# A four-layer graph kernel on one core: the last row tile's products in row quarters of the array, and the degree products behind a conditional

## The chip, the cores and the metric

The kernel runs on one core of a Trainium2 chip. The metric is the device time of one execution in microseconds. The core's engines are named as the profile names them: PE is TensorE's matmul, PEld its weight load, DVE is VectorE, ACT is ScalarE, POOL is GpSimd, and SP is SyncE, which here issues most of the DMA loads. A q behind a name (PEq, SPq) means the engine's instruction sequencer.

## The reference, cut to what matters

The input is x (2708 rows of 256 numbers) and a square adjacency matrix of 2708 x 2708 numbers. Four layers follow, each made of a graph part and a feed-forward part, both added to x. The change touches the graph parts of layers 0, 1 and 2.

```python
# layer 0: a weight from every adjacency value
msg = layernorm(x) @ W + B
sens = exp(-(1/adj - 1)**2 / (2 * 0.5**2))
x = x + where(adj < 1, sens, 0) @ msg
# layer 1: an adjacency matrix that is scaled by the row sums on both sides
A = adj + eye
D = 1 / sqrt(sum(A, axis=1))
x = x + relu((A * D[:, None] * D[None, :]) @ (layernorm(x) @ W) + b)
# layer 2: attention over the neighbours
h = layernorm(x) @ W.T
s = where(scores > 0, scores, 0.2 * scores)   # scores = a_src[None, :] + a_dst[:, None]
e = exp(s) * (adj > 0)
x = x + elu((e / sum(e, axis=1)) @ h)
```

The feed-forward parts of layers 0 and 1 send rows to experts: two of eight in layer 0, one of eight in layer 1. Layer 3 has attention with four heads.

## The kernel before

**Tiles.** The 2708 rows are cut into 22 row tiles of 128; the last one, number FULL = 21, has only LAST = 20 rows. Q is 32, a quarter of the array. The adjacency matrix is read transposed (adjT), so that a block of 128 source rows and 128 target columns can stand as the stationary operand of a product.

**The graph parts.** In layers 0 and 1 the target tiles are taken in three groups (GROUPS of 9, 7 and 6 tiles, GROUPS1 of 8, 8 and 6; the last group's sixth is the target tile of 20 columns, which last_sums does for itself, in column quarters of the array). A group keeps its sums in PSUM, two target tiles to a bank (acc). A loop over the source row tiles j loads one stretch of adjT (adrow, five buffers in layer 0 and four in layer 1), makes weights of it, and multiplies each target tile's 128 columns with the 256 values of that row tile: msg in layer 0 (line 726), sup in layer 1 (line 942). In layer 0 the weights come from the helper weigh (line 699): three ScalarE activations and two VectorE instructions over the whole stretch. In layer 1 VectorE also writes the mask of nonzero entries (line 919) that layers 2 and 3 use. Layer 2 takes its target tiles in groups of 5, 5, 5, 4 and 2, one PSUM bank each; VectorE makes e from a row of factors, a column of factors G and the mask (line 1133), and TensorE multiplies it with hh, 257 columns wide (line 1136).

The row tile j = 21 goes through the same loop as the others, as its last step, with 20 rows in place of 128. After the loop the sums are read out of PSUM and added to x: line 748 in layer 0, grow (lines 907 to 913) in layer 1, result (line 1078) and a later grow in layer 2.

**The front of a layer.** In layer 0 front(t0) loads two row tiles of x and makes msg for them; it is called for every second j of the first group. In layer 1 norm_project goes through the row tiles in sets of 2, 4, 4, 4, 4 and 4 (FOURS): both loads the experts' outputs of layer 0 and adds them to x (line 846), stats and shift make mean and scale, ScalarE normalises, TensorE transposes and projects, and ScalarE scales the result by deg into sup (line 897). The tiles of both share their buffers with the adjacency rows of layer 1.

**The degrees.** While layer 0's experts run, VectorE adds up the adjacency rows into cs (line 784). Twenty-two products with a column of ones turn cs into deg (line 791), each followed by a VectorE copy (line 792). Before layer 1's front VectorE adds 1 and takes 1/sqrt by a shift and three Newton steps (rsqrt, line 147; called in line 851).

**The conditional.** The experts' rows are run in blocks. Fifteen of layer 0's later blocks always run; the rest stand in a conditional (run_rest, line 563), which in this data is not entered. Each engine takes its own branch there, and what follows the conditional and depends on work in it waits until the engine concerned has passed.

**The order of the work.** The framework traces the kernel and sets each engine's order of instructions by itself, by its own estimate of when each can start and by program order. Each engine then runs its own queue strictly in that order, SP's and POOL's too, so that a DMA that waits holds up those behind it. Where the author wants another order, a dependency without a semaphore is added by hand (tc.add_manual_dep with NoSync). A ScalarE activation through lnexp is tied in this way to the table of exp and log that pin loads.

The softmax here doesn't subtract the row's maximum and nothing guards it: scores larger than these inputs give would overflow.

## Time and profile before

| what | value |
|---|---|
| time of three runs, median (lowest to highest) | 2094.61 us (2092.79 to 2096.02) |
| the profiled execution: its own time | 2098.78 us |
| the profiled execution: span from first to last instruction | 2097.1 us |
| mean TensorE clock granted in it | 0.965 |
| products of the last row tile in layers 0, 1, 2 | 21 each |
| TensorE busy, its longest idle stretches | 1980.9 us; 13.3 us at 660, 10.7 us at 1210, 8.8 us at 2076, 8.7 us at 311, 7.9 us at 258 |
| DMA: bytes moved, mean rate | 226.64 MB, 108 GB/s |

The profile shows one execution on the chip. Its page gives each engine's busy time, the span in 40 slices, and groups of instructions by line, engine and operation, with the tiles they write and read. A float32 product appears as two records of PE and two of PEld. In a row of a group, the figures behind the count are the busy time in us and the mean duration of one record in ns, and behind the bar stands the engine's idle time before them with what ended it. In a row of waits the three figures are the total in us, the number and the longest. In a row of an engine's timeline the first figure is the start in us, the second the length.

### The profile page before, as it was taken

The numbers are of one execution on the slowest core, as the hardware profiler recorded it, in microseconds if no ns is written. First come the engines' busy times: TensorE is split into PE (matmuls) and PEld (weight loads), VectorE is DVE, ScalarE is ACT, GpSimd is POOL, SyncE is SP. The second block draws the span as 40 slices with busy tenths as digits, with TensorE's granted clock in tenths as the row PEclk, the third lists the DMA queues.
The fourth block names the chain that finished last, engine by engine and source line by source line (L and its number), as shares of the span: only waits on it lengthen the run. The fifth ranks groups of instructions, "written<-read, shape, count | busy, mean of one in ns | idle before, by whom it ended". The sixth has DMA issues, their size and how long they took to land.

```text
span 2097.1 us, 25890 instructions
## 1 busy us (share of the span) xinstructions
PE 1980.9 (94%) x9673; PEld 1424.7 (68%) x9673; DVE 1100.6 (52%) x2524; ACT 660.6 (31%) x1445; POOL 288.1 (14%) x315
## 2 busy tenths in 40 slices
PE   6999978999997999999899969999899999999997
PEld 5888767878885788878688848888566622232334
DVE  7677754544114323243331165455355488887876
ACT  7778732222222403022322351223243410120112
POOL 1004353333221000102142110000000000000000
PEclk9999989999997999999999989999899999999999
DMA  8435649987532442423265420000101000000000
GB/s 261 141 106 150 213 158 353 352 298 262 186 145 92 123 142 61 141 62 111 92 213 184 162 91 6 1 1 1 41 1 31 16 1 21 21 26 11 16 11 24
DMA packets 80611, 226.64 MB, mean 108 GB/s; under 512 B 15218, under 2 KB 38746, under 8 KB 71264
## 3 DMA queue, kind: packets, MB, share of 16 engines
q1 hardware_dynamic: 69056, 196.17, 28.4%
q0 software_dynamic: 11424, 28.74, 3.9%
q8 instruction: 80, 1.31, 0.3%
q14 instruction: 51, 0.42, 0.1%
HBM read 206.46 MB, written 20.65 MB: 108 GB/s over the span
## 4 chain that ended last, share of the span: by engine, by line
PE 57%; DMA 5%; issue 3%; DVE 2%; ACT 1%; POOL 1%; POOLq 0%; SPq 0%; DVEq 0%; ACTq 0%
PE num L1460 11%; PE ps_acc L1136 10%; PE acc L942 9%; PE ps_tmp L317 7%; PE den L1471 6%; DMA given<-ys,xs 4%; PE ps_acc L1312 3%; PE ps_tmp L238 3%; PE ps_acc L547 1%; PE ps_tmp L195 1%; PE ps_acc L238 1%; PE yacc L556 1%; PE ps_tmp L874 1%; DMA mine<-given 0%; POOL given L451 0%
## 5 line engine op out<-in xcount | busy, mean ns | idle before, releaser
L1455 DVE SCALAR_TENSOR_TENSOR e<-arena,G,mask 128x1024 f32<-128x1024 f32 (+2 forms) x264 | 294.1, 1149 | 44.0 <-PE den L1471 43.6
L556 PE MATMUL yacc<-wb,hTs 128*128 128x256 f32 x1152 | 267.5, 385 | 11.2 <-DVE ys L558 10.7
L556 PEld LDWEIGHTS yacc<-wb,hTs 128*128 128x128 f32 x1152 | 218.0, 193 | 44.0 <-DVE ys L558 14.6
L1460 PE MATMUL num<-e,wh 128*64 128x512 f32 (+4 forms) x1056 | 243.6, 558 | 0.0
L726 PE MATMUL acc<-msg,wt 128*128 128x256 f32 (+1 forms) x924 | 210.7, 386 | 7.9 <-DVE wt L704 7.9
L942 PE MATMUL acc<-sup,adrow 128*128 128x256 f32 (+1 forms) x924 | 214.4, 390 | 0.0
L1136 PE MATMUL ps_acc<-hh,e 128*128 128x257 f32 (+1 forms) x924 | 211.2, 386 | 0.0
L726 PEld LDWEIGHTS acc<-msg,wt 128*128 128x128 f32 (+1 forms) x924 | 175.7, 193 | 35.9 <-DVE wt L704 8.3
L942 PEld LDWEIGHTS acc<-sup,adrow 128*128 128x128 f32 (+1 forms) x924 | 176.6, 195 | 30.6 <-issue 5.5
L1136 PEld LDWEIGHTS ps_acc<-hh,e 128*128 128x128 f32 (+1 forms) x924 | 173.8, 193 | 29.6 <-issue 2.5
L547 PE MATMUL ps_acc<-xTs,wa 128*128 128x256 f32 x768 | 179.6, 385 | 8.7 <-DVE xTs L520 8.6
L1460 PEld LDWEIGHTS num<-e,wh 128*64 128x64 f32 (+1 forms) x1056 | 74.3, 138 | 155.2 <-issue 120.8
L549 ACT ACTIVATE hTs<-ps_acc,wa 128x256 f32<-128x256 f32 x192 | 89.9, 473 | 271.5 <-PE yacc L556 194.4
L547 PEld LDWEIGHTS ps_acc<-xTs,wa 128*128 128x128 f32 x768 | 142.1, 192 | 36.4 <-DVE xTs L520 11.4
L196 ACT COPY xT<-ps_tmp 128x256 f32<-128x256 f32 x126 | 43.0, 362 | 325.1 <-PE ps_tmp L195 324.0
L1471 PE MATMUL den<-e,wh 128*32 128x512 f32 (+4 forms) x1056 | 137.9, 551 | 0.0
L1133 DVE SCALAR_TENSOR_TENSOR e<-Rb,G,mask 128x640 f32<-128x640 f32 (+2 forms) x110 | 85.2, 775 | 97.1 <-PE ps_acc L1136 96.9
L451 POOL DMA_INDIRECT taken<-xr,r_ix x66 | 76.8, 1163 | 357.9 <-DVE b_vec L387 190.7
L451 POOL DMA_INDIRECT given<-ys,xs x72 | 81.8, 1136 | 229.9 <-DVE ys L559 166.0
L465 POOL DMA_INDIRECT xs<-taken,b_ix x72 | 87.2, 1212 | 189.0 <-DVE xTs L520 87.2
L919 DVE TENSOR_SCALAR mask<-adrow 128x1024 uint8<-128x1024 f32 (+1 forms) x66 | 41.6, 631 | 134.5 <-DMA adrow<-in_adjT 132.6
L558 DVE TENSOR_TENSOR ys<-yacc,wb 128x256 f32<-128x256 f32 x72 | 30.3, 421 | 155.2 <-PE yacc L556 155.0
(388 smaller groups left out, 2459.7 us busy)
## 6 DMA issues: line engine op xcount, KB each, us to landing
adhalf<-in_adjT SPq DMA_DIRECT2D x42, 677.0 KB
wb<-in_L_ffn_W2p SPq DMA_DIRECT2D x24, 1152.0 KB
wb<-in_L_ffn_Wdp SPq DMA_DIRECT2D x24, 1152.0 KB
wa<-in_L_ffn_W1b SPq DMA_DIRECT2D x24, 1028.0 KB
adrow<-in_adjT SPq DMA_DIRECT2D x42, 512.0 KB
adrow<-in_adjT SPq DMA_DIRECT2D x42, 320.0 KB
adrow<-in_adjT SPq DMA_DIRECT2D x21, 576.0 KB
adrow<-in_adjT SPq DMA_DIRECT2D x21, 448.0 KB
```

What stands on the lines that cost most here:

```text
L317: te.matmul(p[:, :w], lhsT=w1[:, c, f * P : (f + 1) * P], rhs=xnT[:, c, c0 : c0 + w], start=(c == 0), stop=(c == DC - 1))
L451: i = g.indirect_dma_start(out=dst, out_offset=bass.IndirectOffsetOnAxis(ap=ix, axis=0), in_=src, in_offset=None, bounds_check=bound, oob_ ...
L465: i = g.indirect_dma_start(out=dst, out_offset=None, in_=src, in_offset=bass.IndirectOffsetOnAxis(ap=ix, axis=0), bounds_check=bound, oob_ ...
L547: te.matmul(p[:, f % 2, :], lhsT=w1[:, c, f * P : (f + 1) * P], rhs=xT[:, c, :], start=(c == 0), stop=(c == DC - 1))
L549: s.activation(hT[:, f, :], p[:, f % 2, :], AF.Gelu, bias=bias[:, f : f + 1])
L556: te.matmul(q[:, k, :], lhsT=hT[:, f, k * P : (k + 1) * P], rhs=w2[k][:, f, :], start=(f == 0), stop=(f == HC - 1))
L726: te.matmul(p[:q, n - pair[0], :], lhsT=wt[:, k : k + q], rhs=msg[:r, j, :], start=(j == 0 and n == pair[0]), stop=(j == NT - 1 and n == p ...
L942: te.matmul(p[:q, n - pair[0], :], lhsT=ad[:, k : k + q], rhs=sup[:r, j, :], start=(j == 0 and n == pair[0]), stop=(j == NT - 1 and n == p ...
L1136: te.matmul(p[:q, : D + 1], lhsT=e[:r, k : k + q], rhs=hh[:r, j, :], start=(j == 0), stop=(j == NT - 1))
L1455: v.scalar_tensor_tensor(e[:r, :w], Rb[:r, k, :w], G[:r, j, 2 * pair + k, :], mask[:r, j, c0 : c0 + w], op0=ALU.max, op1=ALU.mult)
L1460: te.matmul(num[k * DK : (k + 1) * DK, hf, :q], lhsT=wh[:r, j, 2 * pair + k, :DK], rhs=e[:r, h0 - c0 : h0 - c0 + q], start=(j == 0), stop= ...
L1471: te.matmul(den[z : z + Q, :q], lhsT=wh[:ri, i, 2 * pair + k, DK : DK + 1].to_broadcast([ri, Q]), rhs=e[:ri, h0 - c0 : h0 - c0 + q], start ...
```

## The change

The last row tile is taken out of the common loop's shape. Its 20 rows are laid into the four row quarters of the array (rows 0, 32, 64 and 96), so that products of different target tiles, in different PSUM banks, stand in different quarters.

- spread_out copies the 20 rows of values to all four quarters, by four small products with the identity and one ScalarE copy. It is called for msg, for sup, and for hh and G.
- last_rows sets a tile to ones by a GpSimd memset and loads the 20 adjacency rows into quarters of it by DMAs on SP.
- last_product is one product in a row quarter; by_turns orders the target tiles so that neighbours lie in different banks.
- In layer 0 the last rows' weights and products stand in the middle of a group: ahead of row tile 19 in the first group, and of row tile 12 in the other two. The weights are taken over 384 or 256 columns of 128 partitions in place of 1152, 896 or 640 columns of 20. The front of the last two row tiles is called two steps earlier.
- In layers 1 and 2 they stay the last step of a group, with all rows of the mask filled.
- The degree products are ordered behind the conditional. They write one bank (a second one for the last tile), and ScalarE makes 1/sqrt(1 + d) as exp(-0.5 ln(1 + d)).
- In layer 1's front, the additions of a set's expert outputs are ordered behind the shift of the set before.

```diff
-        v.scalar_tensor_tensor(nb, st[0][:, :, 0], -1.0, st[1], op0=ALU.mult, op1=ALU.mult)
+        i = v.scalar_tensor_tensor(nb, st[0][:, :, 0], -1.0, st[1], op0=ALU.mult, op1=ALU.mult)
+        shifts.append(i.ins.name)
...
+    def spread_out(values):
+
+        n = values.shape[1]
+        p = ps_tmp()
+        for z in range(0, P, Q):
+            te.matmul(p[z : z + Q, :n], lhsT=ident[:LAST, :Q], rhs=values[:LAST, :], start=True,
+                      stop=True, tile_position=(0, z))
+        s.copy(values, p[:, :n])
+
+    def last_rows(dst, parts):
+
+        g.memset(dst, 1.0)
+        for q, k, c0, w in parts:
+            nc.sync.dma_start(dst[q * Q : q * Q + LAST, k : k + w],
+                              a["adjT"][FULL * P :, c0 : c0 + w])
+
+    def last_product(p, q, weights, k, values, stop=True):
+        te.matmul(p, lhsT=weights[q * Q : q * Q + LAST, k : k + P],
+                  rhs=values[q * Q : q * Q + LAST, : p.shape[1]], start=False, stop=stop,
+                  tile_position=(q * Q, 0))
+
+    def by_turns(own):
+
+        return [(n, t, k) for z in range(2) for n, (t, k, _) in enumerate(own) if n % 2 == z]
...
-            for j in range(NT):
+
+            places = {n: (n // 2 % 4, n // 8 * 2 + n % 2) for n in range(len(own))}
+            begin = tiles is GROUPS[0]
+            for j in range(FULL):
...
-                if tiles is GROUPS[0] and j % 2 == 0:
-                    front(j)
+                if begin and j % 2 == 0:
+                    for t0 in (j,) if j < FULL - 3 else (j, j + 2) if j == FULL - 3 else ():
+                        front(t0)
+                if begin and j == FULL - 2:
+                    spread_out(msg[:, FULL, :])
+                if j == (FULL - 2 if begin else 12):
+                    cols = [gp.tile([P, GMAX * P], F32, name=name, tag=name, bufs=bufs)[
+                        :, : (1 + max(k for _, k in places.values())) * P]
+                            for name, bufs in (("adrow", 5), ("y", 3), ("wt", 4))]
+                    last_rows(cols[0], [(places[n][0], places[n][1] * P, c0 + n * P,
+                                         min(2, len(own) - n) * P) for n in range(0, len(own), 2)])
+                    weigh(*cols, P)
+                    for n, t, _ in by_turns(own):
+                        last_product(acc[n // 2][:, n % 2, :], places[n][0], cols[2],
+                                     places[n][1] * P, msg[:, FULL, :], False)
...
-        for t in range(NT):
-            r = rows(t)
+
+        for q, t0, t1 in ((P, 0, FULL), (LAST, FULL, NT)):
             d = ps_tmp()
-            te.matmul(d[:r, :1], lhsT=cs[:, t * P : t * P + r], rhs=ones, start=True, stop=True)
-            v.tensor_copy(deg[:r, t : t + 1], d[:r, :1])
+            for t in range(t0, t1):
+                i = te.matmul(d[:q, t : t + 1], lhsT=cs[:, t * P : t * P + q], rhs=ones,
+                              start=(t == t0), stop=(t == t1 - 1))
+
+                tc.add_manual_dep(i.ins, scattered["given0"][-1].name, mybir.DependencyInfo(
+                    mybir.DependencyClass.NoSync, mybir.DependencyReason.DATA), reason="order")
+            lnexp(deg[:q, t0:t1], d[:q, t0:t1], AF.Ln, bias=ones[:q])
+        lnexp(deg, deg, AF.Exp, scale=-0.5)
...
-                        v.tensor_tensor(xs, xs, o[:r, some[0] - t0 : some[-1] + 1 - t0,
-                                                  k * D : (k + 1) * D], ALU.add)
-
-
-        v.tensor_scalar(deg, deg, 1.0, None, op0=ALU.add)
-        deg = rsqrt(tp, deg, NT)
+                        i = v.tensor_tensor(xs, xs, o[:r, some[0] - t0 : some[-1] + 1 - t0,
+                                                      k * D : (k + 1) * D], ALU.add)
+                        if shifts:
+
+                            tc.add_manual_dep(i.ins, shifts[-1], mybir.DependencyInfo(
+                                mybir.DependencyClass.NoSync, mybir.DependencyReason.DATA),
+                                reason="order")
...
+                if j == FULL:
+
+                    r = P
+                    if tiles is GROUPS1[0]:
+                        spread_out(sup[:, FULL, :])
                 ad = gp.tile([P, 8 * P], F32, name="adrow", tag="adrow", bufs=4)[:r, :w]
-                nc.sync.dma_start(ad, a["adjT"][j * P : j * P + r, c0 : c0 + w])
+                if j < FULL:
+                    nc.sync.dma_start(ad, a["adjT"][j * P : j * P + r, c0 : c0 + w])
+                else:
+                    last_rows(ad, [(q, 0, c0, w) for q in range(P // Q)])
...
+                if j == FULL:
+                    for n, t, k in by_turns(own):
+                        last_product(acc[n // 2][:, n % 2, :], n // 2, ad, k, sup[:, FULL, :],
+                                     n == pairs[n // 2][-1])
+                    continue
...
+            spread_out(hh[:, FULL, :])
+            spread_out(G[:, FULL, :])
...
-                    r = rows(j)
+                    r = P
...
-                    for (t, k, q), p in zip(own, acc):
-                        te.matmul(p[:q, : D + 1], lhsT=e[:r, k : k + q], rhs=hh[:r, j, :],
-                                  start=(j == 0), stop=(j == NT - 1))
+                    for n, ((t, k, q), p) in enumerate(zip(own, acc)):
+                        if j == FULL:
+                            last_product(p[:, : D + 1], n % 4, e, k, hh[:, FULL, :])
+                        else:
+                            te.matmul(p[:, : D + 1], lhsT=e[:, k : k + q], rhs=hh[:, j, :],
+                                      start=(j == 0), stop=False)
```

## The prediction, made before the result was known

> **What bounds the kernel now.** I began with the page's busy shares and its 40 slices.
>
> ```profile
> PE 1980.9 (94%) x9673; PEld 1424.7 (68%) x9673; DVE 1100.6 (52%) x2524; ACT 660.6 (31%) x1445; POOL 288.1 (14%) x315
> PE   6999978999997999999899969999899999999997
> PEclk9999989999997999999999989999899999999999
> ```
>
> TensorE is the bound nearly everywhere; its thin slices (6th, 13th, 24th, 29th, counted from 1) are the joints between stages. So I priced TensorE's time stage by stage, then asked at each joint what comes last. Next, the groups of instructions with shapes kept apart: the last row tile's products, and two of the products that already lie in column quarters.
>
> ```profile
> L726 PE MATMUL acc<-msg,wt 20*128 20x256 f32 x42 | 9.9, 383 | 0.0
> L942 PE MATMUL acc<-sup,adrow 20*128 20x256 f32 x42 | 10.9, 410 | 0.0
> L1136 PE MATMUL ps_acc<-hh,e 20*128 20x257 f32 x42 | 10.4, 387 | 0.0
> L256 PE MATMUL acc<-sup,adlast 128*32 128x256 f32 x42 | 2.8, 381 | 0.0
> L256 PE MATMUL ps_tmp<-hh,es 128*32 128x257 f32 x42 | 4.4, 529 | 0.0
> ```
>
> Two records are one product. 21 products on 20 rows take about 10 us, though they do a sixth of the work; 21 in column quarters take 2.8. The last row, the same work, takes 4.4. Fine windows (columns: stretch, its length, PE, PEld, DVE, ACT, POOL busy, clock, DMA) say why:
>
> ```profile
> 781.70:785.10 3.40, 3.40 (x16) 2.67 (x16) 2.55 (x4) 0.00 (x0) 0.00 (x0) 1.00 0.55 158
> 785.10:791.90 6.80, 6.80 (x17) 4.91 (x16) 6.80 (x16) 0.00 (x0) 0.00 (x0) 0.50 0.27 80
> 1358.60:1362.00 3.40, 3.40 (x16) 2.43 (x14) 2.09 (x10) 0.96 (x3) 0.00 (x0) 1.00 0.00 0
> 1362.00:1365.40 3.40, 3.40 (x8) 2.73 (x9) 3.16 (x12) 3.40 (x11) 0.00 (x0) 0.50 0.00 0
> ```
>
> The first and third stretch hold the last row tile's products at the end of a group. Right behind them the clock is 0.50, for 6.8 and 3.4 us, although TensorE was never idle. The same follows at 126.3, 904.6, 1307.4 (this slows the 4.4 us row) and 1413.2: 27.2 us at half clock, 13.6 us lost. Full rate is 3.40/16 = 0.2125 us per record, so 0.43 a product.
>
> Third, the joint of layers 0 and 1: SP's waits, the conditional's instructions, TensorE's timeline.
>
> ```profile
> SPq L56 <- DMA given<-ys,xs: 41.5, 1, 41.5
> SPq L56 <- PEq L565: 5.9, 1, 5.9
> ```
> ```profile
> L565 PEldq COMPARE_BRANCH  x2: 328/1992/3657, 660.2 to 1206.9; - x2
> L565 PEldq EVENT_SEMAPHORE  x2: 51/51/51, 664.0 to 1210.2; - x2
> ```
> ```profile
> 653.27 6.71 PE L791 MATMUL ps_tmp<-ones,cs 128*128 128x1 f32 x36 [0.24 <-DVE deg L792]
> 673.30 0.69 PE L195 MATMUL ps_tmp<-ident,xn 128*128 128x128 f32 x2 [13.32 <-ACT xn L207]
> ```
>
> TensorE does the degree products until 660.0, takes its branch at 660.2 (3.66 us), passes at 664.0, and only then SP loads the expert outputs; the scattered rows had landed 5.9 us before. TensorE then idles 13.32 us.
>
> **What the Trainium skill says.** "TensorE: Matmul & The Clock Gate", Part 3: K=32 products at different row positions run beside each other, four measured at 3.07 times one; a weight load overlaps a running product only if the row group differs. The trace has column quarters only: 21 products of 0.43 in 2.71 us, 3.3 times; it agrees for columns, and shows nothing for rows. "TensorEngine Tiling (Array Packing)", Key Properties: changing the mode drains TensorE; between the den and num products of layer 3 this costs 0.13 us (16 records, four steps of 0.43, took 1.85). The first page, Part 1, gives idleness as the cause of a half clock; the trace differs: a busy array with 20 rows in use gets it too. "Runtime: NRT & Kernel Launch", Instruction fetch mechanics: a taken branch outside the loaded window waits for a fetch; the 3.66 us agrees.
>
> **The change, part by part.**
>
> Products: per group the longest quarter holds 3, 2, 2 (layer 0, of 9, 7, 5), 2, 2, 2 (layer 1, of 8, 8, 5) and 2, 2, 2, 1, 1 (layer 2, of 5, 5, 5, 4, 2): 21 steps for 63 products, 42 x 0.43 = 18.1 us less. Bounds: from all four beside each other to none; I take all, as for columns. Each of 11 runs adds a mode change in and out, 0.26. Each spreading copy of 256 columns adds 0.43 + 0.26 = 0.7; its ScalarE copy (362 ns in L196's row) lies beside products. The quarters fill 80 rows for about 1 us, so I expect no half clock. Now by stage.
>
> Layer 0, group 1: 9 products 3.9 become 1.3 + 0.26, half a 3.5 us slow stretch returns 1.75, spreading takes 0.7: 3.4 less. Group 2: 3.0 becomes 1.1: 1.9 less. The narrower weights relieve ScalarE and VectorE, which have cover (75 and 72 us of 95). Group 3 ends on a DMA: its last rows come behind the expert weights in SP's queue, and ScalarE waits 9.73 us for them until 261.5; TensorE then does ten products in 6.4 us, at half clock. Behind the landing only five remain, 4.3 us, 2.1 less; the gathers for the experts come next, so I count 1.5. The weights' issue hangs on group 2's end and moves with it. Layer 0: 6.8.
>
> What moves: the last two tiles' front in group 1 goes from the last step but one to two steps sooner, with its two column loads (about 0.4 us each on SP; the rows of x were read long before, by 34 us) ahead of two adjacency loads, and some 2.2 us of VectorE work; with five row tiles buffered this costs nothing, and without that cover 1 to 2 us once. The last rows' own load and weights leave each group's end for its middle. In layers 1 and 2 VectorE now works on 128 instead of 20 rows, at the same price (L1133: 884 against 872 ns at 640 columns).
>
> The memsets: 204 ns for 128 columns, 314 for 260, so about 1.0 us for 1024; the four or five added loads, 0.35 us each on SP. Queued behind them on SP: the next rows' loads. Five buffers (four in layer 1) are some 10 us ahead, so I count nothing; without that cover each run costs 3 to 5 us.
>
> Degrees: TensorE ends the experts' outputs 0.5 earlier, at about 652.2, its branch runs meanwhile, and the last scatter, free of the degree copies, goes 0.6 earlier. SP then starts at 658.2 - 0.6 = 657.6 instead of 664.1: 6.4. The 22 products take 22 x 0.37 = 8.1 us (36 records in 6.71) in TensorE's idle time, and three ScalarE instructions about 0.8: done near 662, while the first sup comes near 669. Twenty-two copies and the VectorE root are off the path. Ordering: in the old order an addition that waits 0.95 for its load (0.69 itself) stands before the first group's last statistics; this returns 1.5. It gives back: additions now wait for the shift, a chain of about 6 us per four tiles against 5 or less, so the layer's first adjacency loads, in buffers shared with those tiles, come 2.8 earlier and not 7.9. In the 5.1 between, TensorE does 2.6 tiles of front (1.95 each) of 1.09 us work: 2.8. Joint: 5.6.
>
> Layer 1: in L910's records the four bank reads start at 783.2, 784.5, 786.3 and 788.1. Old boundary: 781.7 to 791.9 for the last products and the next row. New: all banks stop at 782.8, the fourth is read by 788.5, its products end 789.4: 2.5 less, twice. The end gives 0.3, spreading takes 0.7: 4.6.
>
> Layer 2: first boundary 1304.0 to 1311.2, 7.3, becomes 1.1 + 2.8: 3.4. Second and third: 6.2 each become 4.8, bound by the banks' reads: 2.8 together. Last two 0.4; two spreadings 1.1: 5.5.
>
> Sum: 6.8 + 5.6 + 4.6 + 5.5 = 22.5. The profiled execution took 2098.8 (span 2097.1): 2076.3. It lies 4.2 above the median of the runs, 2094.6; on that, 2072.
>
> **The rivals.**
>
> Half packing: the two passes of one product hold the next back, so two at a time. 63 x 0.215 = 13.5 instead of 9.0: 2076.5. For it: no row position is in the trace. Against: four column quarters start within 0.02 us.
>
> The clock stays: TensorE waits some 3 us at layer 1's boundaries and 1 in layer 2, enough for half clocks again. Four stretches of 3.4, half lost, 7 with layer 1's second window: 2079.
>
> No packing: products take their turns. What remains is the joint, 5.6, against 11 x 0.26 + 3.2 of spreading: 2094, no change.
>
> Slower: a memset stands on GpSimd behind indirect DMAs that wait for VectorE. GpSimd's timeline has such stretches in just these groups:
>
> ```profile
> 170.88 1.20 POOL L451 DMA_INDIRECT taken<-xr,r_ix  x1 [22.63 <-issue]
> 970.87 1.62 POOL L451 DMA_INDIRECT taken<-xr,r_ix  x1 [101.74 <-DVE b_nb L398]
> ```
>
> If layer 0's second memset, due near 150, goes behind the scatters that end at 199.8, SP's loads stop and TensorE runs dry from about 165: some 40 us, 2112. It decides once GpSimd delays a memset by more than the 10 us cover; at 23 us over the cover the gain is gone. Against: the memset's buffer is free 20 us before these scatters.
>
> **How the numbers follow.** Forecast 0.62 (own range 2062 to 2080: layer 0's end may give 2.4 more, the joint 2.3 more or 2 less, boundaries 3 either way); half packing 0.11, clock 0.13, no packing 0.06, slower 0.08. The range 2061 to 2086 leaves out the last two and the forecast's tails. A measurement of this kernel tells about 0.2%, 4 us, from no change: faster 0.86, same 0.06, slower 0.08.
>
> **What would show it.** Last-row groups with 21 products in some 3 us; clock 1.00 behind group ends; SP's first expert-output load at about 6 us behind the last scatter, no wait for PEq; VectorE's grow as the new wait at layer 1's boundaries. I am wrong if row quarters start one after another, if GpSimd's memsets end what SP waits for, or if the additions' new order holds the front.

## The result, and the profile after

The kernel after took 2085.78 us (median of four runs, 2082.76 to 2086.45) beside 2093.73 us for the kernel before: a ratio of 0.9958, with a 95% interval of 0.994 to 0.9975. That is 8 us less. The forecast was 22.5 us less. Measured again, with 22 executions beside 52, the same two kernels gave 0.998 (0.9967 to 0.9993), 4 us less. So the change is a small gain, a fifth to a third of the forecast.

The page of the kernel after, the first two of the rows shown before:

```profile
PE 1954.2 (94%) x9705; PEld 1403.3 (67%) x9705; DVE 1092.2 (52%) x2490; ACT 659.0 (32%) x1452; POOL 298.6 (14%) x321
PE   6999878999997999999899969999899999999997
```

TensorE is 27 us less busy, yet the spans of these two executions differ by 12.5 (2097.1 and 2084.6). So it waits more. The groups of instructions say that the products themselves did what was forecast (columns as before):

```profile
L286 PE MATMUL acc<-msg,wt 20*128 20x256 f32 x42 | 3.8, 409 | 0.5 <-ACT msg L276 0.5
L286 PE MATMUL acc<-sup,adrow 20*128 20x256 f32 x42 | 3.4, 401 | 0.6 <-issue 0.6
L286 PE MATMUL ps_acc<-hh,e 20*128 20x257 f32 x42 | 4.8, 420 | 0.0
L259 PE MATMUL ps_tmp<-hh,es 128*32 128x257 f32 x42 | 2.8, 382 | 0.0
```

The 63 last products take 12.0 us in place of 31.2. The mean of one record is as long as before (401 to 420 ns), and the sum of a group is a third to a half: the records lie over each other. These are the forecast's own sums: 7, 6 and 8 steps of 0.43 us, with 0.26 for each of 3, 3 and 5 runs, make 3.8, 3.4 and 4.7. The last row of the fence took 4.4 us before, because it fell into a half-clock stretch. The fine windows behind the first group's end of layer 1, and behind that of layer 2 (columns: stretch, its length, the busy time of PE, PEld, DVE, ACT and POOL, the clock, the DMA share, GB/s):

```profile
775.60:779.00 3.40, 3.02 (x7) 2.49 (x8) 3.40 (x7) 0.00 (x0) 0.00 (x0) 0.50 0.62 184
779.00:782.40 3.40, 3.40 (x17) 2.96 (x17) 3.40 (x6) 0.00 (x0) 0.00 (x0) 1.00 0.00 0
1299.80:1303.20 3.40, 3.40 (x49) 1.70 (x45) 3.09 (x15) 2.62 (x8) 0.00 (x0) 1.00 0.00 0
1303.20:1306.60 3.40, 2.73 (x11) 1.45 (x10) 3.40 (x15) 3.40 (x13) 0.00 (x0) 1.00 0.00 0
```

In layer 2 the clock stays at 1.00; in layer 1 one window of 3.4 us at half clock is left of two. The joint of layers 0 and 1, from the timeline:

```profile
646.39 6.58 PE L838 MATMUL ps_tmp<-ones,cs 128*128 128x1 f32 x44 [0.76 <-PEq L595]
651.46 21.44 SPq L56 DMA_DIRECT2D both<-given  x11
659.09 0.69 PE L198 MATMUL ps_tmp<-ident,xn 128*128 128x128 f32 x2 [6.12 <-ACT xn L210]
```

SP starts its loads 4.7 us behind the start of the last scatter (646.76), while TensorE is still at the degree products, and TensorE's idle stretch ahead of layer 1 is 6.12 us where it was 13.32. All this is as forecast. (The 6 us among the prediction's signs was a slip: its own sum, SP at 657.6 and the scatter at 653.2, gives 4.4.) Four waits were not forecast.

First, the end of layer 0, in the kernel after and then in the kernel before:

```profile
240.21 0.35 SPq L650 DMA_DIRECT2D wa<-in_L_ffn_W1b  x1
242.60 2.29 SPq L748 DMA_DIRECT2D adrow<-in_adjT  x2
259.43 0.83 ACT L141 ACTIVATE y<-adrow,tiny 128x640 f32<-128x640 f32 x1 [11.27 <-DMA adrow<-in_adjT]
264.18 5.97 PE L772 MATMUL acc<-msg,wt 128*128 128x256 f32 x20 [10.51 <-DVE wt L734]
```
```profile
266.25 6.46 PE L726 MATMUL acc<-msg,wt 128*128 128x256 f32 x20 [7.91 <-DVE wt L704]
```

Behind the experts' weights SP still issues two row tiles, now tiles 19 and 20 where it was 20 and 21. Ten products (20 records) still follow the landing, and in these two executions TensorE restarts 2.1 us earlier than before (266.25), not 6.8.

Second, the second group's end of layer 1. The lines are the last products, VectorE's first read of a bank (L964), its first xr (L182; xr is the tile of normalised rows for the feed-forward part), and TensorE's transposes of xr; first in the kernel after, then in the kernel before (there the first line is a row of a group):

```profile
890.75 1.15 PE L286 MATMUL acc<-sup,adrow 20*128 20x256 f32 x16
891.92 1.29 DVE L964 TENSOR_TENSOR o<-acc,deg 128x512 f32<-128x512 f32 x2 [1.16 <-PE acc L286]
905.62 2.67 DVE L182 TENSOR_SCALAR xr<-x,mv,rs_y 128x256 f32<-128x256 f32 x8 [0.24 <-DVE rs_y L158]
906.09 1.11 PE L198 MATMUL ps_tmp<-ident,xr 128*128 128x128 f32 x4 [3.19 <-DVE xr L182]
```
```profile
L942 PE MATMUL acc<-sup,adrow 20*128 20x256 f32 x16 | 4.2, 418 | 0.0
902.68 0.69 DVE L910 TENSOR_TENSOR o<-acc,rs_y 128x512 f32<-128x512 f32 x1 [1.16 <-PE acc L942]
916.58 2.68 DVE L182 TENSOR_SCALAR xr<-x,mv,rs_y 128x256 f32<-128x256 f32 x8 [0.31 <-DVE rs_y L158]
918.41 0.60 PE L195 MATMUL ps_tmp<-ident,xr 128*128 128x128 f32 x4
```

VectorE's chain from the first read to xr is 13.7 us after and 13.9 before: no shorter. Nor does it start sooner. Before, the last products start at 901.52 and run one after another; VectorE reads the first bank 1.16 us later, when that bank's two products are done and the others still run. After, all four banks are done at once, and the first read comes 1.17 us behind the start of the products. So the packing shortens TensorE's part by 3 us and leaves VectorE's where it was.

Before, TensorE was still at products when xr was ready (no wait at 918.41). After, it is through with them and waits 3.19 us, and the clock is half from 905.3 to 912.1. The half clock of the kernel before, from 904.6 on, had hidden a part of this wait: the kernel with layer 0's change alone (below), whose layer 1 is as before, met no half clock at this group's end and waited 1.79 us for xr already.

Third, the third group's end, after and then before:

```profile
989.19 0.66 PE L548 MATMUL turned<-ident,xs 128*128 128x128 f32 x4
989.29 1.29 DVE L964 TENSOR_TENSOR o<-acc,deg 128x512 f32<-128x512 f32 x2 [2.98 <-PE acc L286]
996.24 0.65 DVE L550 COPY xTs<-turned 128x512 f32<-128x512 f32 x1
996.94 4.79 PE L577 MATMUL ps_acc<-xTs,L_ffn_W 128*128 128x256 f32 x12 [7.10 <-DVE xTs L550]
```
```profile
998.58 0.69 DVE L910 TENSOR_TENSOR o<-acc,rs_y 128x512 f32<-128x512 f32 x1 [4.34 <-PE acc L942]
1005.63 0.65 DVE L520 COPY xTs<-turned 128x512 f32<-128x512 f32 x1
1006.33 3.78 PE L547 MATMUL ps_acc<-xTs,L_ffn_W 128*128 128x256 f32 x8 [5.78 <-DVE xTs L520]
```

The rows gathered for the experts are there in time; TensorE has turned them before 990. It waits for VectorE's copy of the turned rows, which stands in VectorE's queue behind this group's reads, growing and statistics: 6.95 us from the first read to the copy after, 7.05 before. It is the same pattern as at the second group's end. (An expectation below speaks of a wait for the gathered rows; the lines show otherwise.)

Fourth, layer 1's experts, after and then before:

```profile
1050.82 1.01 POOL L481 DMA_INDIRECT given<-ys,xs  x1 [0.30 <-issue]
1053.45 0.49 DVE L537 MEMSET xs<- 128x516 f32 x1 [7.40 <-DMA given<-ys,xs]
1054.45 0.68 DVE L550 COPY xTs<-turned 128x512 f32<-128x512 f32 x1
1055.18 1.79 PE L577 MATMUL ps_acc<-xTs,L_ffn_W 128*128 128x256 f32 x4 [3.17 <-DVE xTs L550]
```
```profile
1062.13 1.13 PE L547 MATMUL ps_acc<-xTs,L_ffn_W 128*128 128x256 f32 x4 [0.46 <-DVE xTs L520]
```

VectorE stands at a memset until a scatter of GpSimd has ended, with the copy that TensorE needs behind it. Before, that wait of TensorE was 0.46 us. (The scatter comes late because six other indirect DMAs stand ahead of it on GpSimd.)

One profiled execution has its own luck with the clock, so I set the stages beside each other over all profiled executions of this study whose code in that stage is that of the kernel before, or that of the kernel after (2 to 4 and 5 to 10 executions). "Half" is what the half clock costs (half of TensorE's busy time in such stretches), "work" is the rest of its busy time. Differences, after less before, in us:

| stage | length before -> after | difference | idle | half | work | forecast |
|---|---|---|---|---|---|---|
| start to the first expert product of layer 0 | 280.0 -> 276.9 | -3.1 | +6.8 | -4.9 | -4.9 | -6.8 |
| layer 0's experts | 374.7 -> 374.5 | -0.2 | +1.6 | -1.6 | -0.2 | 0 |
| to the first transposes of layer 1 | 19.9 -> 13.5 | -6.4 | -6.4 | +0.2 | -0.2 | with the next two |
| layer 1's graph part | 325.4 -> 328.0 | +2.6 | +6.4 | +0.5 | -4.4 | |
| layer 1's experts | 210.2 -> 216.1 | +5.9 | +4.0 | +2.1 | -0.2 | -10.2 for the three |
| to the first product of layer 2 | 46.6 -> 47.4 | +0.8 | +0.1 | +0.8 | 0 | with the next |
| layer 2's products | 215.6 -> 212.4 | -3.2 | +3.1 | -3.0 | -3.4 | -5.5 for the two |
| to layer 3's products | 199.5 -> 199.8 | +0.3 | +0.8 | -0.4 | -0.1 | 0 |
| layer 3's products (unchanged) | 397.9 -> 395.0 | -2.9 | 0 | -3.1 | +0.1 | 0 |
| to the end | 24.6 -> 25.2 | +0.6 | +0.4 | +0.2 | 0 | 0 |

The sum is -5.6 us, between the two measured differences. TensorE's work fell by 13.3 us; the forecast's own terms say 18.1 - 11 x 0.26 - 2.5 = 12.7. The clock returned 9.2. But TensorE's idle time grew by 23 us outside the joint. In the first row idle time took more than the saved work (6.8 for 4.9); what is left there is clock, and the three executions before stand anywhere between 276.1 and 283.6.

### The profile page after: what moved, and what is told of

Read it like the earlier page. It is cut to its first block, busy times and chain, and to the rows that moved or that the text cites. A ratio compares the mean times of both kernels' runs of the same rounds, so it can differ in the third digit from the quotient of the medians.

```text
span 2084.6 us, 25984 instructions
## 1 busy us (share of the span) xinstructions
PE 1954.2 (94%) x9705; PEld 1403.3 (67%) x9705; DVE 1092.2 (52%) x2490; ACT 659.0 (32%) x1452; POOL 298.6 (14%) x321
## 4 chain that ended last, share of the span: by engine, by line
PE 38%; DMA 5%; issue 3%; DVE 2%; ACT 1%; POOL 1%; POOLq 0%; DVEq 0%; SPq 0%; ACTq 0%
PE num L1532 11%; PE ps_acc L1208 9%; PE den L1543 6%; DMA given<-ys,xs 4%; PE ps_tmp L347 4%; PE ps_acc L1384 3%; PE ps_tmp L241 2%; PE ps_acc L241 1%; PE ps_tmp L198 1%; DMA mine<-given 0%; POOL given L481 0%; POOL xs L495 0%; DVE e L1202 0%; PE ps_tmp L1461 0%; DMA arena<-rows 0%
## 5 line engine op out<-in xcount | busy, mean ns | idle before, releaser
L586 PE MATMUL yacc<-wb,hTs 128*128 128x256 f32 x1152 | 266.8, 384 | 12.5 <-DVE ys L588 12.4
L586 PEld LDWEIGHTS yacc<-wb,hTs 128*128 128x128 f32 x1152 | 217.0, 192 | 45.4 <-DVE ys L588 17.1
L772 PE MATMUL acc<-msg,wt 128*128 128x256 f32 x882 | 199.5, 383 | 12.4 <-DVE wt L734 11.7
L1009 PE MATMUL acc<-sup,adrow 128*128 128x256 f32 x882 | 200.5, 385 | 1.5 <-DVE o L964 1.5
L1208 PE MATMUL ps_acc<-hh,e 128*128 128x257 f32 x882 | 199.2, 382 | 1.7 <-ACT o L1153 1.7
L772 PEld LDWEIGHTS acc<-msg,wt 128*128 128x128 f32 x882 | 165.8, 191 | 38.7 <-DVE wt L734 13.0
L1009 PEld LDWEIGHTS acc<-sup,adrow 128*128 128x128 f32 x882 | 166.5, 192 | 28.8 <-issue 4.5
L1208 PEld LDWEIGHTS ps_acc<-hh,e 128*128 128x128 f32 x882 | 163.7, 190 | 29.3 <-ACT o L1153 4.7
L481 POOL DMA_INDIRECT given<-ys,xs x72 | 87.7, 1218 | 229.1 <-DVE ys L589 163.0
```

Source lines behind the costliest of these rows:

```text
L481: i = g.indirect_dma_start(out=dst, out_offset=bass.IndirectOffsetOnAxis(ap=ix, axis=0), in_=src, in_offset=None, bounds_check=bound, oob_ ...
L586: te.matmul(q[:, k, :], lhsT=hT[:, f, k * P : (k + 1) * P], rhs=w2[k][:, f, :], start=(f == 0), stop=(f == HC - 1))
L772: te.matmul(p[:q, n - pair[0], :], lhsT=wt[:, k : k + q], rhs=msg[:r, j, :], start=(j == 0 and n == pair[0]), stop=(j == FULL - 1 and n == ...
L1009: te.matmul(p[:q, n - pair[0], :], lhsT=ad[:, k : k + q], rhs=sup[:r, j, :], start=(j == 0 and n == pair[0]), stop=False)
L1208: te.matmul(p[:, : D + 1], lhsT=e[:, k : k + q], rhs=hh[:, j, :], start=(j == 0), stop=False)
```

## The experiments

Two theories stood against each other. **Next wait**: the products are as short as forecast, and the gain of layers 0 and 1 goes into waits for other engines and transfers that were nearly as late. **Clock**: the gain is there and half-clock stretches elsewhere eat it. For single parts, others were possible, as their expectations say.

**One layer at a time.** The first three kernels are the kernel before with one part of the change: the hunks of layer 0's loop, those of degrees and ordering, and those of layer 1's loop.

> The kernel before with the change of layer 0 alone. By the prediction's step (6.8 us less in layer 0) TensorE's first expert product comes near 269 us instead of 276.1, and the time falls by 6 to 7 us. Theory 'next wait' (two row tiles still stand behind the experts' weights in SP's queue, and the landing of those weights sets the end of group 3): the stall at the end of group 3 ends near 264, the first expert product comes 2 to 3 us earlier, and the time falls by 2 to 3 us. Theory 'clock' (the gain is there and is lost to half-clock stretches elsewhere): the first expert product comes 5 us or more earlier and some later stage is longer at half clock.

Measured: ratio 0.9983 (0.9969 to 0.9997): 3.6 us less, 0.6 to 6.5 by the interval, which holds the 2 to 3 of "next wait" and leaves the step's 6.8 just outside. The stall at the end of group 3 is 11.8 us, where the three executions with layer 0 as before have 7.9 to 8.4: it takes back a good part of the saved work. It ends at 266.8, not near 264. The first expert product comes at 277.7, beside 283.6 and 280.3 in the next two kernels, which have layer 0 as before and ran on the same chip, but also beside 276.1 in the kernel before. Executions of the same code differ by up to 7.5 us by then, so the profiles do not say how much of the 6.8 is left.

> The kernel before with the joint of layers 0 and 1 alone (degree products behind the conditional, root by ScalarE, order of the additions). Prediction's step: 5.6 us less. Theory 'clock': the first transposes of layer 1 come 7 us earlier, but the clock stays half until some 14 us into the front, so that about 2 us are left at the first group's end. Theory 'order' (the additions, tied to the shift, hold the front): as much is lost, but at full clock, as waits for VectorE. If neither loses anything, 5 to 8 us remain at the end of layer 1's first group.

Measured: ratio 0.9982 (0.9971 to 0.9993), 3.8 us less, and 1.5 to 6.1 by the interval: the forecast's 5.6 lies inside. In its profile the first transposes come 7.0 us nearer to the experts' end, and the graph part behind them is 5.1 to 7.3 us longer (331.6 beside 326.5 and 324.3 with this part as before), with 5.8 us more of half clock and no more idle time. In this execution, the slowest of its 22, the clock gave the gain back. That the joint's change causes it is not shown: the two executions with this part as before stand 5 us of half clock apart (9.4 and 4.4), and five of the full change have 4.9 to 10.4.

> The kernel before with the change of layer 1 alone. Prediction's step: 4.6 us less, 2.5 at each of two group ends. Theory 'next wait': the row-quarter products are as short as priced, but at the second group's end TensorE now waits about 3 us for VectorE's xr, at the third for the gathered rows, and in layer 1's experts some 3 us for VectorE, so that at the end of layer 1's experts 0 to 1 us are left. Theory 'clock': the waits do not come, and 4 to 5 us are left there unless a half-clock stretch falls between.

Measured: ratio 1.0012 (0.9996 to 1.0028), between 0.8 us less and 5.9 more; a gain of 4.6 lies outside. Its trace has the wait of 3.19 us at the second group's xr, one of 7.09 us for VectorE's copy at the third group's end (5.78 before) and 1.86 us at the memset in the experts. The graph part is as long as before (324.8), the experts take 214.0 in place of 210.2.

**Row quarters or not.** In layer 2 all last products are put into one row quarter:

```diff
-                            last_product(p[:, : D + 1], n % 4, e, k, hh[:, FULL, :])
+                            last_product(p[:, : D + 1], 0, e, k, hh[:, FULL, :])
```

> The kernel after, with layer 2's 21 last products all in row quarter 0 in place of four (everything else as in the kernel after). If products in different row quarters run beside each other, these 21 take 9 us and more instead of 4.8, a half clock may follow the first group's end as in the kernel before, and the time is 4 to 7 us above the kernel after, some 2 to 4 us under the kernel before. If the row quarters are worth nothing by themselves, the time stays within 1 us of the kernel after, 8 us under the kernel before.

Measured: ratio 1.0008 (0.9992 to 1.0025), which is some 6 to 10 us above the kernel after by its two comparisons; 4 to 7, and so a time under that of the kernel before, were expected. The group's row:

```profile
L286 PE MATMUL ps_acc<-hh,e 20*128 20x257 f32 x42 | 10.4, 387 | 0.0
```

10.4 us in one quarter, just what it took in the kernel before, and 4.8 in four: products in different row quarters do lie beside each other, those in one don't. Layer 2's products take 217.0 us in place of 212.4, with a half clock of 3.4 again, and with 0.1 us of idle time in place of 3.2. The other 1 to 5 us lie outside this stage. The packing itself is shown.

**The end of layer 0.** The experts' weights are held behind the last adjacency row in SP's queue:

```diff
...
+            for i in (i1, i2):
+                tc.add_manual_dep(i.ins, loads[-1], mybir.DependencyInfo(
+                    mybir.DependencyClass.NoSync, mybir.DependencyReason.DATA), reason="order")
...
+                loads.append(i.ins.name)
...
-                if end and j == NT - 5:
+                if end and j == FULL - 1:
...
```

> The kernel after, with the experts' first weights held behind the last adjacency row in SP's queue (layer 0, group 3). Theory 'next wait' (the landing of 4.4 MB of weights, queued ahead of two row tiles, sets the end of group 3): TensorE's stall of 10.5 us at the end of group 3 shrinks to under 4 us, the last products end near 256 instead of 270, the first expert product comes 5 to 10 us earlier than in the kernel after, and the time falls by as much less whatever the second block's weights then cost. If something else sets the stall (the rows' own transfer, ScalarE's weights), the first expert product comes no earlier than in the kernel after.

Measured: ratio 0.9941 (0.9922 to 0.996). The last adjacency products end at 258.6 without a stall, and the first expert product comes at 271.9, 5.0 us ahead of the mean of the kernel after (276.9). But most of the stall only changed its name:

```profile
257.64 0.98 POOL L481 DMA_INDIRECT taken<-xr,r_ix  x1 [0.30 <-issue]
264.64 0.21 POOL L693 COPY xr<-choice 128x12 int32<-128x12 int32 x1 [6.02 <-DMA taken<-xr,r_ix]
265.43 1.08 POOL L495 DMA_INDIRECT xs<-taken,b_ix  x1 [0.58 <-issue]
270.04 1.11 PE L548 MATMUL turned<-ident,xs 128*128 128x128 f32 x4 [11.39 <-DMA xs<-taken,b_ix]
```

Now TensorE waits 11.39 us for the gathered rows: GpSimd's scatters (taken) go out until 258.6, they land by 264.6, and only then the gather (xs) is issued. Two chains ended within 5 us of each other; taking away the first shows the second.

**Layer 1's group ends.** The last rows are taken in the middle of a group, as in layer 0 (MID is 12):

```diff
-            for j in range(NT):
+            for j in [*range(MID), FULL, *range(MID, FULL)]:
...
-                        last_product(acc[n // 2][:, n % 2, :], n // 2, ad, k, sup[:, FULL, :],
-                                     n == pairs[n // 2][-1])
+                        last_product(acc[n // 2][:, n % 2, :], n // 2, ad, k, sup[:, FULL, :], False)
...
```

> The kernel after, with layer 1's last rows taken in the middle of a group (ahead of row tile 12), so that the banks end one after another with products of 128 rows. Theory 'next wait' (all four banks end within 1.2 us, so that VectorE reads and grows all of them before it comes to the statistics, and TensorE, ahead by 2.5 us, runs dry at xr): the waits of 0.7 us at the banks and of 3.2 us at the second group's xr go, the group ends hold TensorE less, and layer 1's graph part is 3 to 5 us shorter than in the kernel after. If instead VectorE's load as a whole is what holds TensorE there, the wait at xr stays and the stage is as long as in the kernel after, within 1 us.

Measured: ratio 0.9997 (0.9983 to 1.0012): the gain is gone. The waits of 0.7 us are gone too, and that at the second xr is 1.93 us; but the graph part is 338.7 us long, 10.7 more: 4.3 of idle time, 3.4 of half clock and 2.9 of work. These are lines of the third group:

```profile
963.46 1.63 POOL L482 DMA_INDIRECT taken<-xr,r_ix  x1 [104.77 <-DVE b_nb L429]
973.33 0.98 POOL L482 DMA_INDIRECT taken<-xr,r_ix  x1 [0.30 <-issue]
974.30 0.66 POOL L281 MEMSET adrow<- 128x640 f32 x1
974.98 1.42 SPq L283 DMA_DIRECT2D adrow<-in_adjT  x4
977.39 2.04 PE L287 MATMUL acc<-sup,adrow 20*128 20x256 f32 x4 [6.74 <-DMA adrow<-in_adjT]
```

The memset of 0.66 us stands behind eight indirect DMAs of GpSimd, 1.3 us each; SP's loads wait for it, with the next rows behind them, and TensorE stands still for 6.74 us. This is the prediction's slower rival, in a kernel that puts the memset where the change does not. The experiment is no clean answer to the question it was made for.

**VectorE's chain.** The root of layer 1's row statistics is taken by ScalarE in place of VectorE's shift and Newton steps:

```diff
             t0 = tiles[0]
-            st = stats(tiles)
+            st = stats(tiles, by_log=True)
             xr = gt.tile([P, GM, XW], F32, name="xr", bufs=1)[:, :G]
```

> The kernel after, with the root of layer 1's row statistics (ahead of xr) taken by ScalarE as exp(-0.5 ln) in place of the shift and three Newton steps of VectorE, which take 2.4 us at each group end. Theory 'next wait' (VectorE's chain from the last read of the banks to xr sets the stall of 3.2 us at the second group's end): the chain gets some 1.5 us shorter, the wait at xr falls to 1.5 to 2 us and layer 1's graph part is 1 to 3 us shorter, by the half clock behind the wait too. If something else holds xr (the adjacency rows, the masks), the wait stays at 3.2 us.

Measured: ratio 0.9947 (0.9928 to 0.9965), 11 us under the kernel before and 7.6 under the kernel after measured beside it (2081.9 and 2089.5), more than was expected. The waits at the second xr and in the experts both answer:

```profile
903.84 0.30 ACT L141 ACTIVATE var<-mv,eps 128x8 f32<-128x8 f32 x1 [67.52 <-DVE adlast L296]
904.88 0.77 PE L198 MATMUL ps_tmp<-ident,xr 128*128 128x128 f32 x4 [1.40 <-DVE xr L182]
...
1050.23 1.13 PE L577 MATMUL ps_acc<-xTs,L_ffn_W 128*128 128x256 f32 x4 [1.76 <-DVE xTs L550]
```

The wait at xr is 1.40 us in place of 3.19, with no half clock behind it; the graph part takes 322.4 us in place of 328.0, the experts 211.9 in place of 216.1. From the first read of a bank to the first xr VectorE now takes 11.5 us (892.94 to 904.41) in place of 13.7. So a cut of 2.2 us in VectorE's chain takes 1.8 us off the wait at xr: "next wait" is shown here. The size of the gain is less sure. Of the 9.8 us by which the two stages are shorter some 4 are idle time and some 6 half clock, and executions of the same code differ by as much half clock.

**The memset in the experts.** It goes from VectorE to GpSimd, in layer 1 alone:

```diff
-                v.memset(xs, 1.0)
+                (g if n == 2 else v).memset(xs, 1.0)
```

> The kernel after, with the memset of the gathered rows' buffer in layer 1's experts on GpSimd instead of VectorE. Theory 'next wait' (at 1052 TensorE waits 3.2 us for the copy of turned rows, which stands on VectorE behind a memset that waits for a scatter's end): this wait goes, with the 1.7 us of half clock behind it, and layer 1's experts take 3 to 5 us less than in the kernel after. If the scatter itself is what is late, TensorE waits elsewhere for the same row block, and the stage is as long as before.

Measured: ratio 0.9959 (0.9946 to 0.9972), not to be told from the kernel after. The stage is shorter, as expected: 210.7 us in place of 216.1, and the wait is gone:

```profile
1051.83 1.13 PE L577 MATMUL ps_acc<-xTs,L_ffn_W 128*128 128x256 f32 x4
1055.57 0.53 POOL L537 MEMSET xs<- 128x516 f32 x1 [2.13 <-PE yacc L586]
1055.82 1.03 PE L577 MATMUL ps_acc<-xTs,L_ffn_W 128*128 128x256 f32 x4
```

In the same execution layer 3's unchanged products took 401.3 us, 8.3 more than where no half clock falls on them; and it is the slowest of the five that were timed; so what the shorter stage is worth in time is open.

**The front of layer 1.** TensorE is kept busy ahead of it:

```diff
+        for _ in range(4):
+            k = te.matmul(ps_tmp()[:, :W], lhsT=ident, rhs=w_l1.rearrange("p c d -> p (c d)"),
+                          start=True, stop=True)
...
```

> The kernel after, with four products of 512 columns on nothing that is used, behind the degree products, in TensorE's idle 6 us ahead of layer 1's front. Theory 'clock' (the front's first five row tiles run at half clock because TensorE comes out of idleness, 3.3 us more of half clock than in the kernel before): the clock is back at 1.00 by the first or second row tile, these come 2 us apart instead of 3, and the front is some 3 us shorter. Theory 'order' (the additions that wait for the shift set the pace of the front): the front is no shorter at full clock, and TensorE only waits longer between the row tiles. If the products delay the first transposes, up to 1 us is lost.

Measured: ratio 0.9971 (0.9959 to 0.9983), no more than the kernel after.

```profile
657.65 5.26 PE L846 MATMUL ps_tmp<-L_gnn_W,ident 128*128 128x512 f32 x8 [0.23 <-ACT deg L141]
666.55 1.90 DVE L903 TENSOR_TENSOR x<-x,both 128x512 f32<-128x512 f32 x3 [1.24 <-DMA both<-given]
671.79 0.69 PE L198 MATMUL ps_tmp<-ident,xn 128*128 128x128 f32 x2 [2.54 <-ACT xn L210]
```

The clock is back from 660.8 on, and the first two row tiles come 1.9 us apart. Then VectorE waits for a load of the experts' outputs, TensorE waits 2.54 us for the set behind it, and the clock falls again (671.1 to 677.9). The stretch from the first transposes to the first adjacency product is 30.6 us: no shorter than in the other executions with this front (28.1 to 31.8). So the clock alone does not set the front: a load is next in line.

> The kernel after, without the order of the additions behind the shift of the set before (degree products and root as in the kernel after). Theory 'order' (at full clock the additions that wait for the shift set the front's pace; a wait of 2.5 us came to light once the front was kept at full clock): layer 1's first adjacency products start earlier, and transposes to first group end take 2 us less or more. Theory 'clock' alone: without the order the front is as long as before, 110 us from its first transposes to the first group's end; the first transposes come 1 to 1.5 us later because an addition that waits for its load stands in front.

The edit removes the manual dependency of the additions on the shift. Measured: ratio 0.9973 (0.9962 to 0.9985), beside 0.998 (0.9967 to 0.9993) of the unchanged kernel after: not to be told apart. In its profile the first transposes come 1.2 us later, as expected, and the graph part takes 323.7 us in place of 328.0, of which 1.7 are half clock and 1.5 idle. The first adjacency product comes 25.3 us behind the first transposes (28.1 to 31.8 with the order), but by the first group's end nothing is left of it: VectorE's first read of a bank comes 127.3 us behind the experts' end, and 126.8 to 130.4 with the order. So the order gains at the start of the front and gives as much back within it.

**Together, and once more.** The first combines rows_first, log_layer1 and xs_pool.

> The kernel after with three waits taken away together: the experts' first weights behind the last adjacency row (layer 0), the root of layer 1's row statistics by ScalarE, and the memset in layer 1's experts on GpSimd. If the gain of the shorter products was swallowed by these waits, it comes back: some 3 us in layer 0, 1 to 3 in layer 1's graph part, 4 to 5 in its experts, so 8 to 11 us below the kernel after, near 2076 us. If each of them only gives way to a further wait, the time stays within 3 us of the kernel after.

> The kernel after once more, unchanged, on the chip of this call: what a profile of the same code shows again is the code's, what differs is chance. Expected: 6 to 10 us below the kernel before, the waits at the second group's xr (3.2 us) and in layer 1's experts (3.2 us) as in its first profile, and half-clock stretches in other places of layer 0, the front and layer 3, each worth 1.7 us.

Measured: the combination 0.9949 (0.9929 to 0.9969), median 2079.9 us; the kernel after again 0.998 (0.9967 to 0.9993), median 2089.5. The combination beats both kernels, the kernel after by 9.7 us, within the 8 to 11 expected. Its stages: first expert product at 273.4, graph part of layer 1 325.1, experts 209.2 (as short as in the kernel before, for all that TensorE comes earlier). It is not told from log_layer1 or rows_first alone, so it is not shown that the three add up. The kernel after again gained 4 us where 6 to 10 were expected. It shows 3.19 us at the second xr and 3.16 us in the experts, to 0.01 us what its first profile has: those are the code's. Its half clocks in layer 0's experts, in the front and in layer 3 lie elsewhere: those are chance.

## Why the prediction was wrong

The sign was right and the size was not: 8 us, and 4 when measured again, for 22.5. That 2085.8 is inside the stated range, 2061 to 2086, says nothing for the argument: it is above the forecast's own range, which ended at 2080.

- **The products: right.** 21 take 3.8, 3.4 and 4.8 us; TensorE's work fell by 13.3 us for 12.7. Half packing and no packing are ruled out by these rows and by the kernel with one quarter.
- **The clock behind group ends: right in layers 0 and 2**, where the stretches at 126.3, 1307.4, 1362.0 and 1413.2 are gone; in layer 1 only in part: in the first profile one window of two is left behind the first group, and at the second they moved to the wait for xr. The price was read from one execution: the kernel with layer 0's change alone, with layer 1 as before, has one window at the first group's end and none at the second.
- **Layer 1 is the step that failed**: "its products end 789.4: 2.5 less, twice", summed to 4.6. At the group ends themselves it holds: the banks' reads cost TensorE 0.73 and 0.76 us, less than the 3 feared, since VectorE reads two banks before it goes on. But the step stopped there. It named VectorE's grow as the new wait and did not follow VectorE on, through grow, statistics and root to xr: a chain of 13.7 us that starts 1.2 us behind the last products' start in both kernels, so that the change moves neither its start nor its length. TensorE's lead ran into it (3.19 us and the half clock there), then into the like chain to the copy at the third group's end (7.10 us for 5.78), then into the memset in the experts (3.17 for 0.46). Alone, the change of layer 1 makes the time between 0.8 us shorter and 5.9 longer. The kernels with the root on ScalarE and with the memset on GpSimd show what sets the first and the last of these waits; for the wait at the third group's end the order of VectorE's queue is read from the trace and was not tried.
- **Layer 0, 6.8: 3.6 alone** (0.6 to 6.5). "Behind the landing only five remain": ten remain, because SP's order moved by one row tile. And had five remained, the gathered rows stood only some 5 us behind, as the kernel with rows first shows.
- **The joint, 5.6: 3.8 alone** (1.5 to 6.1). The earlier start is 6.4 us where 7.9 were summed. The give-back was named. The half clock, 5.8 us more of it in the one profile with the joint alone, was not, and whether it belongs to the change is open.
- **Layer 2, 5.5: 2.4 by the stages**, with the spreading counted; it was not run alone. The work fell by 3.4 and the clock gave 3.0, but 3.1 us of waits came up. The step had taken the banks' reads as a bound; in the first profile they cost 1.7 of 3.2 us, and other instructions of ScalarE the rest (the read of the last tile's sums 0.7, a normalised row tile 0.6). With one quarter, where the products take 5.6 us longer, these waits are gone: here too the next chain stood close behind.
- **The slower rival** did not come, and its mechanism is real: in the kernel with the last rows in the middle of layer 1's groups it costs TensorE 6.74 us.
- **Two smaller slips** change nothing: the rival without packing counts 3.2 us of spreading where the layers' sums hold 2.5, and a memset of 1024 columns took 1.23 us, not about 1.0.

What stays open: 2.9 us of the mean gain stand in layer 3, whose code is the same. How many half-clock windows fall there goes with the place of the windows' grid at its first product. That product starts 2.1 to 2.4 us behind a window's start in the four executions with layer 2 as before, and each has three half-clock windows; with layer 2 changed it starts 2.99 us or more behind in six, which have none, and 1.7 to 2.6 in four, which have one, three, three and five. The places are nearly the same in all: with one exception some 69, 131 and 202 to 206 us into the stage. Whether the change moves this start against the grid or chance does, no run settles.

## What to carry to other kernels

Where an engine is 94% busy, a saving on it is worth only the slack to the next chain at every joint behind it; ask of each saved microsecond which instruction takes the engine up again, and price the whole chain ahead of that one, not only its first link: when it starts, and whether the change moves that start at all. When a wait goes and another of nearly its length stands in its place, the second was there already: shorten both. Before two profiles are subtracted, split idle, half clock and work by stage, and look at stages that the change doesn't touch: they show how much is chance.

## What the runs showed of the hardware that I had not expected

Layer 3's products, with unchanged instructions and no idle time, took 393.0, 394.6, 398.0 or 401.3 us, by the number of half-clock windows that fell on them (none, one, three and five, of 3.4 us each). Every half-clock stretch away from a trace's end is a multiple of 3.41 us. The grid of these windows stood anywhere from 0.05 to 3.0 us against the start of the program. The Trainium skill ("TensorE: Matmul & The Clock Gate", Part 1) calls this window free-running, and the traces agree; that a stretch on which TensorE is busy throughout is slowed by it is this case's own finding.

Packing ends such half clocks. With layer 2's last products laid into four row quarters its stage had none in any of nine executions; with the same products one behind another it lost 1.7 to 5.1 us to them in four executions of the old code, and 3.4 in the kernel with one quarter.

A memset on GpSimd costs 0.66 us for 640 columns and 1.23 us for 1024. In the queue behind eight indirect DMAs it came 10.8 us after the first of them had started.
